# Attention block on one core: 1/l through ScalarE's queue, sums of the second pair made on VectorE, weights in two tiles, division pinned, v's products in seven of eight steps

## The chip, the core and the metric

The kernel runs on one core of a Trainium2 chip. The core has TensorE (PE, matmuls), VectorE (DVE), ScalarE (ACT), GpSimd (POOL) and SyncE (SP); each works through its own queue of instructions in order, and they wait for each other on semaphores. DMAs are issued by SP, ACT and POOL. Everything is fp32. The metric is device time in microseconds, shorter is better.

## What is computed

x has 16 images of 512 channels and 32 x 32 = 1024 positions. Each image is normalised in 8 groups of channels, goes through self-attention with 4 heads of 128 channels, and a projection is added to x:

```
qkv = jnp.einsum('oc,bchw->bohw', qkv_w, xn) + qkv_b[:, None, None]
q, k, v = jnp.split(qkv, 3, axis=1)          # then to heads: b, head, n, d
attn = jax.nn.softmax(jnp.einsum('bhnd,bhmd->bhnm', q, k) * scale, axis=-1)
out = jnp.einsum('bhnm,bhmd->bhnd', attn, v)  # then back to b, c, h, w
out = jnp.einsum('oc,bchw->bohw', proj_w, out) + proj_b[:, None, None]
return x + out
```

## The kernel before

**The main loop.** An image has four heads, a head eight steps (j = 0 to 7), one for each 128 keys. In step s, `scores` (L709) multiplies the keys' block with all queries in two halves of 512 (L712), ScalarE takes exp (L717), VectorE adds the result to `tot` (L723, L725); `weighted_sum` (L792) multiplies the block of step s - 1 with v (L797). There are 16 x 4 x 8 = 512 steps. After a head's last step ScalarE copies the weighted sum out of PSUM (L804).

**The work between.** All other products are laid into the steps as units, by `plan_head` (L938) and `spread`: in head 0 of an image the q and k of its second pair of heads, in head 1 the projection of the image before and the statistics of the next one, in head 2 the first pair's q and k of the next image, in head 3 the next image's v. Half of a step's units run after each half of the scores. Each of the four is a product of 512 by 512 by 1024 done by Strassen's scheme (its Winograd form) on two levels, in `two_levels` (L457): the outer seven products fall into four groups, `OUTER` (L151), of two, two, two and one. Each group has seven units, one for each inner product in the order 1, 2, 6, 5, 7, 4, 3; the groups start 0, 4, 8 and 16 units from the first (`staggered`, L833), so that two are under way at a time. A unit's matmuls are at L510; ScalarE copies intermediate results (L421, L527), VectorE adds them (L529), combines groups (L565) and finishes q and k (L597), v (L649 and L652, then through DRAM on POOL's queue at L660 and L665) and the projection (L693, L696).

**Inner sums.** A group needs four sums of its right-hand factor, t1 to t4 (`inner_sum`, L486; a subtraction of 128 x 256 at L495 for each of the group's members). For the first pair of heads they are made on VectorE and also written to DRAM (`"keep"`, L499). The second pair and v have the same right-hand factor and load them from there through SP's queue (`"load"`, L484, and `first_loads`, L556, for the first group, called as `ahead[...]` one head earlier). The projection makes its own. There is one tile for each of t1 to t4.

**Weights.** `group_weights` (L345) brings the seven left-hand factors of a group, `[128, 2, 7, 128]`, into one of two buffers of the tag `w`; `SLOTS` (L147) says which factor lies where. In the first image they are made from the given weights and written to DRAM (L376), later loaded from there through SP (L350), 896 KB for a group of two.

**1/l.** When a head is done, `denominators` (L727) takes the sums of `tot` over the keys on VectorE (L732 to L742), writes 1/l as one row of 1024 to DRAM (L744) and reads it back spread over 128 partitions (L746), both on SP's queue; the second waits for the first. `divide` (L806) multiplies the head's output with it on VectorE. It is traced in step 5 of the next head. The divided outputs of an image's heads are added up for the projection (`sums_of_b`, L268, traced in step 6 of the next image's head 0). The very last head is divided in another way (L753).

**What sets the order.** The program is traced in the order of the text, then a planner puts each engine's instructions into a queue: an engine takes the instruction traced first among those that the planner's clock holds to be ready. An instruction can thus stand far from where it was traced. `tc.issue_after(ins)` keeps a block's instructions behind `ins` on its engine.

Of the kernel before, what the change touches and what calls it, by code (L numbers as in the profile page):

```python
# [16 lines left out]
P = 128  # L17
# [126 lines left out]
    5: ("s1", "t1"), 6: ("s2", "t2"), 7: ("s3", "t3"),  # L144
}

SLOTS = {"a11": 0, "a12": 1, "a21": 2, "s3": 2, "a22": 3, "s1": 4, "s2": 5, "s4": 6}  # L147
KC = 2
Q = 256

# [4 lines left out]
def fast_path(ctx, tc, x, sources, out, consts, flag, dims):  # L155
# [157 lines left out]
    stage, store = {}, {}  # L313
    for site in (*range(PAIRS), "proj", "v"):
        for g, group in enumerate(OUTER):
            store[site, g] = kept.tile(
                [P, len(group), 7, P], F32, name=f"kept_{site}_{g}"
            )

    store["last"] = kept.tile([P, 8, HALF], F32, name="kept_last")  # L320

# [22 lines left out]

    def group_weights(site, g, first):  # L345

        group = OUTER[g]
        w = wpool.tile([P, 2, 7, P], F32, tag="w", name=f"w_{site}_{g}")
        if not first:
            nc.sync.dma_start(w[:, : len(group)], store[site, g])  # L350
            return w
        st, raw = stage[site], raw_blocks(site)
        for i, p in enumerate(group):
            n = FACTORS[p][0]
            flat = w[:, i, 0:4, :].rearrange("p s d -> p (s d)")
            if n in raw:
                load_block(w[:, i, 0:4, :], raw[n])
            elif n == "s1":
                nc.vector.tensor_add(flat, st["a21"], st["a22"])
            elif n == "s2":  # L360
                nc.vector.tensor_sub(flat, st["s1"], st["a11"])
            elif n == "s3":
                nc.vector.tensor_sub(flat, st["a11"], st["a21"])
            else:
                nc.vector.tensor_sub(flat, st["a12"], st["s2"])
            if site == "proj":
                nc.sync.dma_start(store["last"][:, p], flat)

        def at(n):
            return w[:, : len(group), SLOTS[n], :]  # L370

        nc.vector.tensor_add(at("s1"), at("a21"), at("a22"))
        nc.vector.tensor_sub(at("s3"), at("a11"), at("a21"))
        nc.vector.tensor_sub(at("s2"), at("s1"), at("a11"))
        nc.vector.tensor_sub(at("s4"), at("a12"), at("s2"))
        nc.sync.dma_start(store[site, g], w[:, : len(group)])  # L376
        return w

    wv = {}
# [77 lines left out]
    def two_levels(name, site, b, blocks, finish, sums="make"):  # L457
# [10 lines left out]
        def group_units(g):  # L468
            group = OUTER[g]
            n = len(group)  # L470
            have = haves[g]

            def weights():
                have["w"] = group_weights(site, g, b == 0 and site in range(PAIRS))

            def sum_tile(h, m):
                haves[h][m] = tpool.tile(
                    [P, 2, Q], F32, tag=f"in_{m}", name=f"{name}_{h}_{m}"
                )
                return haves[h][m][:, : len(OUTER[h])]  # L480

            def load(h, m):
                if sums == "load" and h < len(OUTER):
                    nc.sync.dma_start(sum_tile(h, m), inner_kept[b, h, m])  # L484

            def inner_sum(m):  # L486
                if sums == "load":
                    return
                sum_tile(g, m)
                a, c = {  # L490
                    "t1": ("b12", "b11"), "t2": ("b22", "t1"), "t3": ("t2", "b11"),
                    "t4": ("b21", "t2"),
                }[m]
                for i in range(n):
                    nc.vector.tensor_sub(have[m][:, i, :], inner(i, a), inner(i, c))  # L495
                if sums == "keep":
                    t = dpool.tile([P, n, Q], F32, tag=f"{m}_{g}", bufs=1, name=f"kept_{m}_{g}")
                    inner_kept[b, g, m] = t
                    nc.gpsimd.dma_start(t, have[m][:, :n])  # L499

            def inner(i, m):
                if m[0] == "t":
                    return have[m][:, i, :]
                outer = blocks()[FACTORS[group[i]][1]]
                return outer[int(m[1]) - 1][:, ts(int(m[2]) - 1, Q)]

            def mm(acc, j, first):
                an, bn = FACTORS[j]
                for i in range(n):
                    nc.tensor.matmul(  # L510
                        acc[:, ts(i, Q)], have["w"][:, i, SLOTS[an], :], inner(i, bn),
                        start=(first and i == 0), stop=True, skip_group_check=True,
                    )

            def out_(which, a, c=None):
                row, half = int(which[1]) - 1, int(which[2]) - 1
                if g not in R:
                    R[g] = rpool.tile(
                        [P, 2, 2, HALF], F32, tag=f"r{g % 3}", name=f"{name}_r{g}"
                    )  # L520
                dst = R[g][:, :n, row, ts(half, Q)]

                def view(t):
                    return t[:, : n * Q].rearrange("p (i q) -> p i q", q=Q)

                if c is None:
                    nc.scalar.copy(dst, view(a))  # L527
                else:
                    nc.vector.tensor_add(dst, view(a), view(c))  # L529

            p1, p2, p6, p5, p7, p4, p3 = strassen(f"{name}_{g}", mm, out_, n * Q)

            def unit(*steps):
                def one():
                    for f in steps:
                        f()
                    for _ in range(min(len(pending), 2 if g == len(OUTER) - 1 else 1)):
                        pending.pop(0)()
                return one

            def end():
                combine(g)
                if g == len(OUTER) - 1:
                    run(pending)
                    pending.clear()


            return [
                unit(weights, lambda: inner_sum("t1"), lambda: inner_sum("t2"), p1),
                unit(lambda: inner_sum("t3"), p2), unit(lambda: inner_sum("t4"), p6),  # L550
                unit(lambda: load(g + 1, "t2"), p5), unit(lambda: load(g + 1, "t1"), p7),
                unit(lambda: load(g + 1, "t3"), p4),
                unit(lambda: load(g + 1, "t4"), p3, end),
            ]
# [34 lines left out]
    def qk_groups(b, pair):  # L589

        def finish(which, r, a, c):
            of, half = int(which[1]) - 1, int(which[2]) - 1
            st, h = (qs, ks)[of], 2 * pair + r
            if (b, h) not in st:
                st[b, h] = qkpool.tile([P, N], F32, tag=f"qk{of}", name=f"qk{of}_{b}_{h}")
            i = of * HEADS + h
            nc.vector.scalar_tensor_tensor(  # L597
                st[b, h][:, ts(half, HALF)], a, qkb_sb[:, i : i + 1], c, ALU.add, ALU.add
            )

        return two_levels(
            f"qk_{b}_{pair}", pair, b, lambda: xb[b], finish, "load" if pair else "keep"
        )

    def v_units(b, jj):
# [94 lines left out]


    ps, tot, po, rinv, last_eviction = {}, {}, {}, {}, {}
    steps = B * HEADS * NB

    def where(s):
# [3 lines left out]
    def scores(s, half):  # L709
# [11 lines left out]
        if j == 1:  # L721
            tot[b, h] = lpool.tile([P, N], F32, tag="tot", name=f"tot_{b}_{h}")
            nc.vector.tensor_add(tot[b, h], ps[s - 1], ps[s])  # L723
        else:
            nc.vector.tensor_add(tot[b, h][:, i], tot[b, h][:, i], ps[s][:, i])  # L725

    def denominators(b, h):  # L727

# [11 lines left out]
        nc.vector.transpose(l[:, 3, :], l[:, 2, :])  # L740
        r = lpool.tile([BLK, BLK], F32, tag="r", bufs=2, name=f"r_{b}_{h}")
        nc.vector.reciprocal(r, l[:, 3, :])  # L742
        row = dpool.tile([1, N], F32, tag="row", name=f"row_{b}_{h}")
        nc.sync.dma_start(row.rearrange("o (c i) -> (o c) i", i=BLK), r)  # L744
        rinv[b, h] = lpool.tile([P, N], F32, tag="rinv", name=f"rinv_{b}_{h}")
        nc.sync.dma_start(rinv[b, h], row.to_broadcast((P, N)))  # L746
        worst = lpool.tile([BLK, BLK], F32, tag="worst", name=f"worst_{b}_{h}")
        i = b * HEADS + h
        nc.vector.scalar_tensor_tensor(
            worst, l[:, 3, :], 1.0, r, ALU.mult, ALU.max, accum_out=spans[:, i : i + 1]  # L750
        )

    def last_division(b, h):  # L753

# [183 lines left out]
    def plan_head(b, h):  # L938
# [39 lines left out]
        elif h == 2:  # L978
            spread(plan, staggered(qk_groups(b + 1, 0)), 0, NB)
        else:  # L980
            spread(plan, staggered(next_v.pop()), 0, NB)
        return plan

    def warm(n, name):
# [24 lines left out]
    stage_sums(0)  # L1009
    run(staggered(qk_groups(0, 0)))  # L1010
    next_v, next_qk = [], [qk_groups(0, 1)]
    ahead["qk_0_1"]()
    stage_blocks(1)
    stage_sums(1)

# [1 line left out]
    for s in range(steps + 1):  # L1017
        units = []
        if s < steps:
# [4 lines left out]
            if j == NB - 1 and h > 1 and b + 1 < B:  # L1024
                (next_v if h == 2 else next_qk).append(
                    v_groups(b + 1) if h == 2 else qk_groups(b + 1, 1)
                )
                units.append(ahead[f"v_{b + 1}" if h == 2 else f"qk_{b + 1}_1"])
        if 0 < s < steps and s % NB == 0:
            denominators(*where(s - 1)[:2])  # L1030
        for half in range(NH2):
            if s < steps:
                scores(s, half)
                if half == 0 and j == 5 and s > NB:
                    divide(*where(s - NB)[:2])
            if s > 0:
                weighted_sum(s - 1, half)
            n = (len(units) + 1) // 2
# [137 lines left out]
```

## Time and profile before

| | |
|---|---|
| median of 10 runs | 3350.56 us (3344.01 to 3362.43) |
| profiled execution | 3355.27 us, of it the span 3353.4 us |
| granted TensorE clock, mean | 0.986 |
| ACT busy with exp (L717) | 610.0 us, 1024 of 596 ns |
| DVE busy with `tot` (L725) | 469.6 us, 385 of 1220 ns |
| weights, `w`, `w_v` and `w_proj` (SP) | 180 loads of 896 KB, 60 of 448 KB |
| kept sums for q and k (SP) | 192 loads of 256 KB, 64 of 128 KB |
| row of 1/l, its spread (SP) | 63 of 4 KB, 63 of 512 KB |

The profile is of one execution. Busy times of engines overlap; a line of waits gives the engine and line that waited, whom it waited for, the sum, the number and the longest. In a timeline a row gives start, duration, engine, line, what is written from what, the count, and in brackets the idle time before it and what ended it. The line numbers are those of the kernel before.

### The profile page before, as it was taken

The numbers are of one execution on the slowest core, as the hardware profiler recorded it, in microseconds if no ns is written. First come the engines' busy times: TensorE is split into PE (matmuls) and PEld (weight loads), VectorE is DVE, ScalarE is ACT, GpSimd is POOL, SyncE is SP. The second block draws the span as 40 slices with busy tenths as digits, with TensorE's granted clock in tenths as the row PEclk, the third lists the DMA queues.
The fourth block names the chain that finished last, engine by engine and source line by source line (L and its number), as shares of the span: only waits on it lengthen the run. The fifth ranks groups of instructions, "written<-read, shape, count | busy, mean of one in ns | idle before, by whom it ended". The sixth has DMA issues, their size and how long they took to land.

```text
span 3353.4 us, 33635 instructions
## 1 busy us (share of the span) xinstructions
PE 3221.2 (96%) x10474; PEld 2184.3 (65%) x10474; DVE 2520.2 (75%) x4161; ACT 1437.8 (43%) x2709; POOL 526.0 (16%) x938
## 2 busy tenths in 40 slices
PE   8999999999999999999999999999999999999999
PEld 6566666666666666666666666666666666666664
DVE  7876869768687776877778677786776867778675
ACT  2534435344353443534435353353533535344342
POOL 1011121111211112120121201212012121121100
PEclk9999999999999999999999999999999999999999
DMA  6665564555645456464564645646456474464731
GB/s 226 214 201 176 172 210 162 178 162 171 216 152 184 155 183 200 160 190 150 177 204 152 200 152 173 208 146 212 138 171 204 148 217 149 163 201 156 220 130 45
DMA packets 209527, 589.27 MB, mean 176 GB/s; under 512 B 32960, under 2 KB 64192, under 8 KB 209344
## 3 DMA queue, kind: packets, MB, share of 16 engines
q1 hardware_dynamic: 140080, 368.89, 34.5%
q0 software_dynamic: 67392, 216.07, 19.3%
q10 hardware_dynamic: 1872, 2.11, 0.2%
q8 instruction: 86, 1.41, 0.2%
q14 instruction: 97, 0.79, 0.1%
HBM read 448.28 MB, written 138.67 MB: 175 GB/s over the span
## 4 chain that ended last, share of the span: by engine, by line
PE 65%; DVE 13%; DMA 10%; issue 10%; POOL 1%; ACT 0%; SPq 0%; POOLq 0%; ACTq 0%; DVEq 0%
PE po L797 18%; PE s L712 17%; PE qk_x L510 8%; PE qk_y L510 6%; PE v_x L510 5%; PE v_y L510 4%; PE pp_x L510 3%; DMA w<-kept 3%; PE pp_y L510 3%; DMA rinv<-row 2%; DMA row<-r 2%; DVE xt L272 2%; DMA y<-in_x 1%; DVE tot L725 1%; DVE vt L649 1%
## 5 line engine op out<-in xcount | busy, mean ns | idle before, releaser
L717 ACT ACTIVATE p<-s 128x512 f32<-128x512 f32 x1024 | 610.0, 596 | 1072.9 <-PE s L712 1067.2
L797 PE MATMUL po<-p,v 128*128 128x512 f32 x2048 | 1063.2, 601 | 1.2 <-ACT o L804 1.2
L712 PE MATMUL s<-qk,qk 128*128 128x512 f32 x2048 | 1060.4, 600 | 2.2 <-ACT p L717 1.9
L797 PEld LDWEIGHTS po<-p,v 128*128 128x128 f32 x2048 | 602.3, 303 | 332.1 <-issue 215.8
L725 DVE TENSOR_TENSOR tot<-tot,p 128x1024 f32<-128x1024 f32 x385 | 469.6, 1220 | 115.8 <-ACT p L717 113.6
L712 PEld LDWEIGHTS s<-qk,qk 128*128 128x128 f32 x2048 | 391.2, 192 | 93.4 <-issue 29.7
L510 PEld LDWEIGHTS qk_x<-qk_t,w 128*128 128x128 f32 x1344 | 253.0, 193 | 184.7 <-issue 72.3
L510 PE MATMUL qk_x<-qk_t,w 128*128 128x256 f32 x1344 | 361.8, 386 | 7.2 <-ACT qk_u L421 6.0
L529 DVE TENSOR_TENSOR qk_r<-qk_y,qk_u 128x512 f32<-128x512 f32 (+1 forms) x256 | 158.7, 620 | 164.8 <-ACT qk_u L421 139.2
L421 ACT COPY qk_u<-qk_x 128x512 f32<-128x512 f32 (+1 forms) x256 | 136.1, 532 | 260.4 <-PE qk_x L510 260.4
L499 POOL DMA_DIRECT2D kept_t<-qk_t x256 | 138.2, 540 | 490.2 <-DVE qk_t L495 442.2
L510 PE MATMUL qk_y<-qk_t,w 128*128 128x256 f32 x448 | 134.2, 414 | 75.8 <-DVE qk_r L529 69.8
L660 POOL DMA_DIRECT2D vd<-vu x120 | 66.3, 552 | 805.2 <-DVE vu L652 781.1
L807 DVE TENSOR_TENSOR o<-o,rinv 128x1024 f32<-128x1024 f32 x63 | 77.1, 1223 | 135.8 <-DMA rinv<-row 135.4
L510 PE MATMUL pp_x<-pp_t,w_proj 128*128 128x256 f32 x630 | 173.3, 389 | 0.0
L510 PEld LDWEIGHTS v_x<-v_t,w_v 128*128 128x128 f32 x630 | 118.4, 190 | 79.1 <-issue 38.3
L697 POOL DMA_DIRECT2D out_y<-y x120 | 66.2, 551 | 651.7 <-DVE y L696 619.5
L529 DVE TENSOR_TENSOR v_r<-v_y,v_u 128x512 f32<-128x512 f32 (+1 forms) x120 | 74.7, 623 | 123.4 <-ACT v_u L421 115.8
L510 PE MATMUL v_x<-v_t,w_v 128*128 128x256 f32 x630 | 166.6, 381 | 0.0
L510 PEld LDWEIGHTS qk_y<-qk_t,w 128*128 128x128 f32 x448 | 86.7, 202 | 116.4 <-DVE qk_r L529 75.8
L665 POOL DMA_DIRECT2D v<-vd x240 | 139.8, 590 | 104.1 <-issue 44.1
L510 PEld LDWEIGHTS pp_x<-pp_t,w_proj 128*128 128x128 f32 x630 | 113.9, 190 | 63.7 <-issue 18.9
(204 smaller groups left out, 4358.5 us busy)
## 6 DMA issues: line engine op xcount, KB each, us to landing
w<-kept SPq DMA_DIRECT2D x90, 896.0 KB, 6.2
kept_t<-qk_t POOLq DMA_DIRECT2D x192, 256.0 KB, 3.0
qk_t<-kept_t SPq DMA_DIRECT2D x192, 256.0 KB, 4.6
v_t<-kept_t SPq DMA_DIRECT2D x180, 256.0 KB, 2.7
w_v<-kept_v SPq DMA_DIRECT2D x45, 896.0 KB, 4.9
w_proj<-kept_proj SPq DMA_DIRECT2D x45, 896.0 KB, 4.5
rinv<-row SPq DMA_DIRECT2D x63, 512.0 KB, 4.9
x<-in_x POOLq DMA_DIRECT2D x60, 512.0 KB, 6.0
```

The costliest lines, as they stand in the source:

```text
L272: nc.vector.tensor_sub(b[o][k], b[i][k], b[j][k])
L421: nc.scalar.copy(t[n][:, :width], t["x"][:, :width])
L499: nc.gpsimd.dma_start(t, have[m][:, :n])
L510: nc.tensor.matmul(acc[:, ts(i, Q)], have["w"][:, i, SLOTS[an], :], inner(i, bn), start=(first and i == 0), stop=True, skip_group_check=True,)
L529: nc.vector.tensor_add(dst, view(a), view(c))
L660: nc.gpsimd.dma_start(rows[which][ts(h, P), :], u)
L665: nc.gpsimd.dma_start(vs[b, pair][ts(q, BLK), half].rearrange("m h (k i) j -> m (h k) (i j)", k=n), rows[which].rearrange("(k m) (q e) -> ...
L712: nc.tensor.matmul(sc, ks[b, h][:, ts(j, P)], qs[b, h][:, ts(half, HALF)], start=True, stop=True)
L717: nc.scalar.activation(ps[s][:, ts(half, HALF)], sc, AF.Exp, scale=SCALE)
L725: nc.vector.tensor_add(tot[b, h][:, i], tot[b, h][:, i], ps[s][:, i])
L797: nc.tensor.matmul(po[b, h][:, i], v_block(b, h, j), ps[s][:, i], start=(j == 0), stop=(j == NB - 1),)
L807: nc.vector.tensor_mul(os_[b, h], os_[b, h], rinv.pop((b, h)))
```

## The change

- The two DMAs of 1/l leave `denominators` and SP's queue. A new function, `spread_inverse`, issues them on ScalarE's queue: the row is traced in the first half of step 1 of the next head, the spread in the second half.
- `divide` is traced in the second half of step 4 instead of the first half of step 5, and kept behind VectorE's sum of step 4 on `tot`.
- The second pair makes its inner sums on VectorE (`"make"`) instead of loading them; its `ahead` call is gone. The first pair still writes them out, for v.
- A group's weights lie in two tiles, of four factors (a11, a12, s1, s2, which the products 1, 2, 6 and 5 use) and three (a21 or s3, a22, s4, for 7, 4 and 3), with two buffers each, and are stored and loaded in two DMAs. Where the first image makes them, each 512 wide operation becomes two of 256.
- The units of v in head 3 are laid into steps 0 to 6 instead of 0 to 7.

```diff
-SLOTS = {"a11": 0, "a12": 1, "a21": 2, "s3": 2, "a22": 3, "s1": 4, "s2": 5, "s4": 6}
+SLOTS = {
+    "a11": (0, 0), "a12": (0, 1), "s1": (0, 2), "s2": (0, 3),
+    "a21": (1, 0), "s3": (1, 0), "a22": (1, 1), "s4": (1, 2),
+}
+PARTS = (4, 3)
...
-            store[site, g] = kept.tile(
-                [P, len(group), 7, P], F32, name=f"kept_{site}_{g}"
-            )
+            for t, m in enumerate(PARTS):
+                store[site, g, t] = kept.tile(
+                    [P, len(group), m, P], F32, name=f"kept_{site}_{g}_{t}"
+                )
...
-        w = wpool.tile([P, 2, 7, P], F32, tag="w", name=f"w_{site}_{g}")
+        n = len(group)
+        w = [
+            wpool.tile([P, 2, m, P], F32, tag=f"w{t}", name=f"w{t}_{site}_{g}")
+            for t, m in enumerate(PARTS)
+        ]
         if not first:
-            nc.sync.dma_start(w[:, : len(group)], store[site, g])
+            for t in range(2):
+                nc.sync.dma_start(w[t][:, :n], store[site, g, t])
             return w
...
                 for i in range(n):
                     nc.tensor.matmul(
-                        acc[:, ts(i, Q)], have["w"][:, i, SLOTS[an], :], inner(i, bn),
+                        acc[:, ts(i, Q)], have["w"][t][:, i, slot, :], inner(i, bn),
                         start=(first and i == 0), stop=True, skip_group_check=True,
                     )
...
-            f"qk_{b}_{pair}", pair, b, lambda: xb[b], finish, "load" if pair else "keep"
+            f"qk_{b}_{pair}", pair, b, lambda: xb[b], finish, "make" if pair else "keep"
...
-            nc.vector.tensor_add(tot[b, h][:, i], tot[b, h][:, i], ps[s][:, i])
+            added[b, h, j] = nc.vector.tensor_add(
+                tot[b, h][:, i], tot[b, h][:, i], ps[s][:, i]
+            )
...
-        row = dpool.tile([1, N], F32, tag="row", name=f"row_{b}_{h}")
-        nc.sync.dma_start(row.rearrange("o (c i) -> (o c) i", i=BLK), r)
-        rinv[b, h] = lpool.tile([P, N], F32, tag="rinv", name=f"rinv_{b}_{h}")
-        nc.sync.dma_start(rinv[b, h], row.to_broadcast((P, N)))
+        inverse[b, h] = r
...
+    def spread_inverse(b, h, step):
+
+        if step == 0:
+            row = rows_of[b, h] = dpool.tile([1, N], F32, tag="row", name=f"row_{b}_{h}")
+            nc.scalar.dma_start(
+                row.rearrange("o (c i) -> (o c) i", i=BLK), inverse.pop((b, h))
+            )
+            return
+        rinv[b, h] = lpool.tile([P, N], F32, tag="rinv", name=f"rinv_{b}_{h}")
+        nc.scalar.dma_start(rinv[b, h], rows_of.pop((b, h)).to_broadcast((P, N)))
...
-            spread(plan, staggered(next_v.pop()), 0, NB)
+
+            spread(plan, staggered(next_v.pop()), 0, NB - 1)
...
-    ahead["qk_0_1"]()
...
-                units.append(ahead[f"v_{b + 1}" if h == 2 else f"qk_{b + 1}_1"])
+                if h == 2:
+                    units.append(ahead[f"v_{b + 1}"])
...
-                if half == 0 and j == 5 and s > NB:
-                    divide(*where(s - NB)[:2])
+                if j == 1 and s > NB:
+                    spread_inverse(*where(s - NB)[:2], half)
+                if half == 1 and j == 4 and s > NB:
+
+                    with tc.issue_after(added[b, h, 4].ins):
+                        divide(*where(s - NB)[:2])
```

More of the change, by code (lines that the diff above doesn't have):

```diff
@@ L353, in group_weights, with of, at @@
         for i, p in enumerate(group):
[L354 to L365, printed above, removed]
-            if site == "proj":
-                nc.sync.dma_start(store["last"][:, p], flat)
-        def at(n):
-            return w[:, : len(group), SLOTS[n], :]
+            name = FACTORS[p][0]
+            for t in range(2):
+                rows = w[t][:, i, 0:2, :]
+                flat = rows.rearrange("p s d -> p (s d)")
+                if name in raw:
+                    nc.sync.dma_start(
+                        rows, raw[name][:, ts(t, P)].rearrange("(k p) d -> p k d", p=P)
+                    )
+                    continue
+                def of(m):
+                    return st[m][:, ts(t, 2 * P)]
+                if name == "s1":
+                    nc.vector.tensor_add(flat, of("a21"), of("a22"))
+                elif name == "s2":
+                    nc.vector.tensor_sub(flat, of("s1"), of("a11"))
+                elif name == "s3":
+                    nc.vector.tensor_sub(flat, of("a11"), of("a21"))
+                else:
+                    nc.vector.tensor_sub(flat, of("a12"), of("s2"))
+            if site == "proj":
+                for t in range(2):
+                    nc.sync.dma_start(
+                        store["last"][:, p, ts(t, 2 * P)],
+                        w[t][:, i, 0:2, :].rearrange("p s d -> p (s d)"),
+                    )
+        def at(m):
+            t, slot = SLOTS[m]
+            return w[t][:, :n, slot, :]
         nc.vector.tensor_add(at("s1"), at("a21"), at("a22"))
@@ L375, in group_weights @@
         nc.vector.tensor_sub(at("s4"), at("a12"), at("s2"))
-        nc.sync.dma_start(store[site, g], w[:, : len(group)])
+        for t in range(2):
+            nc.sync.dma_start(store[site, g, t], w[t][:, :n])
         return w
@@ L508, in mm @@
                 an, bn = FACTORS[j]
+                t, slot = SLOTS[an]
                 for i in range(n):
                     nc.tensor.matmul(
-                        acc[:, ts(i, Q)], have["w"][:, i, SLOTS[an], :], inner(i, bn),
+                        acc[:, ts(i, Q)], have["w"][t][:, i, slot, :], inner(i, bn),
                         start=(first and i == 0), stop=True, skip_group_check=True,
@@ L702, in fast_path @@
     ps, tot, po, rinv, last_eviction = {}, {}, {}, {}, {}
+    inverse, rows_of, added = {}, {}, {}
     steps = B * HEADS * NB
@@ L724, in scores @@
         else:
-            nc.vector.tensor_add(tot[b, h][:, i], tot[b, h][:, i], ps[s][:, i])
+            added[b, h, j] = nc.vector.tensor_add(
+                tot[b, h][:, i], tot[b, h][:, i], ps[s][:, i]
+            )
     def denominators(b, h):
@@ L751, in denominators @@
         )
+    def spread_inverse(b, h, step):
[3 more added lines that the diff above has]
+                row.rearrange("o (c i) -> (o c) i", i=BLK), inverse.pop((b, h))
+            )
+            return
+        rinv[b, h] = lpool.tile([P, N], F32, tag="rinv", name=f"rinv_{b}_{h}")
+        nc.scalar.dma_start(rinv[b, h], rows_of.pop((b, h)).to_broadcast((P, N)))
     def last_division(b, h):
```

## The prediction

> **What bounds the kernel now.** I read the page first, for the share of each engine, then the windows by head, then the waits, and last the timeline where the waits are.
>
> ```profile
> PE 3221.2 (96%) x10474; PEld 2184.3 (65%) x10474; DVE 2520.2 (75%) x4161; ACT 1437.8 (43%) x2709; POOL 526.0 (16%) x938
> ```
>
> TensorE is the bound: 3353.4 - 3221.2 = 132 us of the span is all that it is idle. The program repeats one image 16 times and an image has four heads, each with the same count of matmuls. Cutting the timeline at the first exp (L717) of each head gives the stretches; those of image 5, heads 0 to 3 in order, are:
>
> ```profile
> core 0: us, PE busy (x) PEld busy (x) DVE busy (x) ACT busy (x) POOL busy (x), PEclk, DMA share, GB/s
> 1077.00:1134.10 57.10, 51.39 (x163) 34.89 (x163) 35.93 (x55) 18.97 (x34) 12.22 (x22) 0.94 0.67 201
> 1134.10:1184.00 49.90, 49.81 (x167) 34.36 (x167) 42.25 (x79) 33.49 (x70) 6.51 (x11) 1.00 0.39 133
> 1184.00:1236.30 52.30, 49.78 (x163) 33.52 (x163) 43.82 (x78) 19.13 (x34) 9.71 (x18) 1.00 0.53 177
> 1236.30:1285.60 49.30, 49.05 (x163) 34.29 (x163) 35.18 (x48) 19.08 (x35) 5.09 (x9) 1.00 0.59 185
> ```
>
> The first number after the stretch is its length. The same work takes 49.3 us in head 3 and 57.1 us in head 0, and only there is the clock below 1. Over images 1 to 14 the means are 56.7, 50.0, 51.4 and 49.2 us. So the time to be had lies in head 0 (7.5 us each) and head 2 (2.2 us). The waits say what it is:
>
> ```profile
> DVE o L807 <- DMA rinv<-row: 135.4, 40, 9.4
> PE qk_y L510 <- DVE qk_r L529: 70.4, 15, 7.5
> PE qk_x L510 <- DMA w<-kept: 20.1, 22, 2.2
> SPq L744 <- DVE worst L749: 249.5, 47, 20.3
> SPq L746 <- DMA row<-r: 111.3, 50, 6.0
> ACT y L866 <- DMA y<-in_x: 11.9, 4, 6.5
> ```
>
> (Columns: total us, times, longest.) VectorE waits for the spread row of 1/l before its division, and TensorE waits 15 times, about once an image, for a sum of products that stands behind that division in VectorE's queue. In image 5:
>
> ```profile
> 1084.65 0.32 SPq L744 DMA_DIRECT2D row<-r  x1
> 1091.48 0.32 SPq L746 DMA_DIRECT2D rinv<-row  x1
> 1096.97 1.22 DVE L807 TENSOR_TENSOR o<-o,rinv 128x1024 f32<-128x1024 f32 x1 [6.41 <-DMA rinv<-row]
> 1100.76 0.68 DVE L529 TENSOR_TENSOR qk_r<-qk_y,qk_u 128x512 f32<-128x512 f32 x1
> 1100.90 2.08 PE L510 MATMUL qk_y<-qk_t,w 128*128 128x256 f32 x4 [4.49 <-DVE qk_r L529]
> ```
>
> The 4 KB row takes 6.8 us to land and the 512 KB spread another 5.5; the division stands at the head of VectorE's queue for 6.41 us, and TensorE stops for 4.49. After it the clock is low:
>
> ```profile
> 1077.00:1098.00 21.00, 18.20 (x62) 12.50 (x61) 10.64 (x19) 8.22 (x14) 10.16 (x19) 1.00 0.84 228
> 1098.00:1106.00 8.00, 5.10 (x10) 2.93 (x11) 4.51 (x7) 0.60 (x1) 0.99 (x2) 0.57 1.03 331
> 1106.00:1134.00 28.00, 28.00 (x93) 19.36 (x92) 20.68 (x30) 10.16 (x19) 1.06 (x2) 1.00 0.43 144
> ```
>
> (Second last number but one: granted clock, then the DMA engines' share.) The stall sits where the DMA engines are full, and the clock falls to 0.57 with it.
>
> [...] every stall of 3.3 us or more in a head 0 has a half-clock stretch of 3.4 to 10.2 us beside it, and the waits of 1.6 to 2.2 us in head 2 have none. [...] the row's landings on SP: 1.3 us median in heads 1 and 3, 2.1 in head 2, and 3.7 to 6.8 in head 0, where weights and kept sums lie ahead of it. [...]
>
> **The change part by part.** Durations are from the profiled execution, which took 3355.3 us (span 3353.4), 4.7 us above the median of 3350.6; the sum is made against it and taken over to the median by those 4.7.
>
> *1/l through ScalarE, division pinned.* The two DMAs of a head leave SP and go to ACT, traced at step 1; the division can't come before VectorE's sum of step 4. In a head 0, exp of step 1 ends at 7.9 us after its start and r is ready at 7.7. With about 2.1 us for the row and 5 for the spread, 1/l is there by some 16 us; the pin stands at about 30. So VectorE's wait goes, TensorE's with it, and the half clock too. Next late in that head is the weights' load (1.21 us at 1086.68), which the second part moves. Head 0 then looks like head 2 without its weights' wait: 51.4 - 1.6 (its mean idle) = 49.8, so 6.9 us each. In image 15 TensorE stalls 5.32 us in head 0 for another reason (ACT in L866 waits 6.5 us for y), which the change leaves. So 14 x 6.9 = 97 us. The sums of o for the projection follow the division, and even at 38 us they stand ahead of the projection of the next head.
>
> The cost: ACT's issue of the spread waits until the row has landed, and its issue of the row until r is there; exps and the copies of L421 stand behind, and TensorE waits for those. SP's issues take 0.32 us each; the trace has four ACT issues of x at 0.41 to 0.46, so two a head are below 1 us of an engine that is busy 19 to 33 us of 50. The wait isn't shown. Below: nothing, if the row lands before ACT gets there (half a step, about 3 us, lies between the two). Above: what the trace shows of a blocked ACT, 6.5 us of wait in image 15 gave 5.3 us of stall, so some 1.2 us are forgiven and the rest is paid in full. For a wait of up to 2.1 us that is at most 0.9 a head. I take 0.2 for 62 heads, 12 us, since 1.3 to 2.1 is less than half a step.
>
> *Sums of the second pair made.* Gone are 16 loads an image on SP (3.5 MB, all for head 0, just where the DMA engines were full). Added are 28 subtractions in head 0; L495 has them for the first pair at 412 ns, so 28 x 0.41 = 11.5 us of VectorE. [...] Head 0's VectorE goes from 36.0 to 47.5, less what v's tail takes along (L649 and L652 have 3.6 us in head 0): 44 to 47.5. Head 2 makes the same sums with 43.8 us and shows waits of TensorE for them of 5.9 us in 14 times over the run, so below 0.5 an image. I take nothing for it beyond the 49.8; the upper bound is in the rivals.
>
> *Weights in two tiles.* The bytes are the same; 16 more SP issues an image cost SP 5 us of 207, beside the 16 loads that go. The first tile (four products) is free after the fourth product of the group two before, three products earlier than the whole was, and 4/7 of it has to land: it comes 3 units (over 2.5 us) earlier, against waits of at most 2.2. So head 2's mean idle of 1.6 goes: 15 x 1.6 = 24 us. Head 0's is in the 49.8. If SP issues a second tile ahead of a first one, part of it stays.
>
> *v's products within seven of eight steps.* Nothing is added. Step 7 of head 3 then has scores and weighted sums alone, some 3.4 us (4 x 0.86); VectorE gets the 3.6 us of v's tail over before head 0. I put 0.2 on head 3 for the uneven filling, 3 us in all. The preparation of the first image makes its sums in halves of 0.41 instead of 0.68: 1 us.
>
> Sum: - 97 - 24 + 12 + 3 + 1 = - 105, or 3250 against 3355.3, 3246 against the median.
>
> **The rivals.** *VectorE becomes head 0's bound.* For: 47.5 of 49.8 us. Head 2 leaves VectorE 6 us unused outside its weights' wait (49.8 - 43.8); if so much is always lost to waits for products, head 0 takes 53.5: 15 x 3.7 = 55 us more, 3300. Against: v's tail leaves head 0, and head 1 can take what is late.
>
> *The change doesn't do what it says.* The stall lies where DMA share is 1.03; if the spread comes late there too, or VectorE only meets another wait (y<-in_x, L693, 14.2 us in all), half of the 121 goes: about 3305. Against it, the pin lies 8 us after the latest landing seen in a head 0 (21.5).
>
> *Slower: ScalarE waits for the row.* In head 2, r is ready at 11.5 us, exp of step 1 ends at 5.6: if ACT issues in the order of the text, it stands 5.9 us, and 5.9 - 1.2 = 4.7 reach TensorE, 15 x 4.7 = 70. In head 0, the row at SP's 5.1 us gives 3.9, 15 x 3.9 = 58. Heads 1 and 3 (r at 5.4 and 4.9) give none. [...] 30 half-clock stretches of 3.4 us add 1.7 each, 51. In place of my 12: 3246 - 12 + 179 = 3413. It decides from 105 + 12 = 117 us on, 1.9 us a head. Against it: the order of this kernel's queues is a planner's (L807, traced at step 5, stands at step 2 or 3), so ACT's issues may be put where r is expected[...].
>
> **How the numbers follow.** The forecast has 0.58, VectorE's bound 0.18, the half effect 0.10, ScalarE's wait 0.12, no net effect 0.02. A measurement of this kernel can tell about 0.2%, 7 us, from no change. Faster 0.58 + 0.18 + 0.10 = 0.86, same 0.02, slower 0.12. The likeliest case goes from 3212 (both heads at 49.2 and no ACT wait: 14 x 7.5 + 15 x 2.2 = 138) to 3275; the range reaches to 3320 to take in the two smaller gains and leaves ScalarE's wait out.
>
> **What would show it.** Right: no division waits for rinv, head 0 at 50 us with clock 1.00, the row landing in about 2 us on ACT's queue, no TensorE wait for w, VectorE 44 to 47 us in head 0. Wrong: ACT waiting for row or r with TensorE idle behind exp or the copies; TensorE waiting for qk_t or qk_r in head 0 by more than 1 us an image; head 3 longer than 50.

## The result, and the profile after

The changed kernel takes 3298.86 us (median of 9 runs, 3293.81 to 3309.37), against 3349.9 us for the kernel before (31 runs, beside it on the same chips). The ratio is 0.9847, 95% interval 0.9836 to 0.9859: 51 us faster, where 105 were forecast. The profiled execution took 3300.64 us, its span is 3298.9 us. Page, shares of the engines:

```profile
PE 3202.4 (97%) x10474; PEld 2178.3 (66%) x10474; DVE 2639.8 (80%) x4625; ACT 1444.0 (44%) x2709; POOL 525.1 (16%) x938
```

The stretches of image 5, heads 0 to 3, as shown of the kernel before:

```profile
core 0: us, PE busy (x) PEld busy (x) DVE busy (x) ACT busy (x) POOL busy (x), PEclk, DMA share, GB/s
1066.80:1120.10 53.30, 50.93 (x163) 34.42 (x163) 43.38 (x77) 18.68 (x34) 11.20 (x21) 0.97 0.55 156
1120.10:1169.70 49.60, 49.22 (x165) 34.10 (x165) 41.86 (x83) 34.15 (x70) 6.00 (x11) 1.00 0.39 123
1169.70:1224.40 54.70, 51.98 (x165) 34.97 (x165) 44.81 (x80) 19.07 (x35) 10.24 (x19) 0.97 0.53 179
1224.40:1274.10 49.70, 49.08 (x163) 34.14 (x163) 34.73 (x50) 19.26 (x35) 6.86 (x12) 1.00 0.55 175
```

Head 0 has fallen, but not to 50, and head 2 has not fallen (this one is the longest of its kind). The means over images 1 to 14 are 52.6, 49.7, 51.75 and 49.7 us, against 56.7, 50.0, 51.4 and 49.2. The waits of the changed kernel that answer to those of before (division and exp now at L846 and L746, the matmuls of the units at L538):

```profile
ACT qk_u L448 <- DVE worst L777: 47.0, 14, 3.6
...
ACT p L746 <- DVE qk_t L522: 42.8, 16, 4.5
...
PE qk_x L538 <- DVE qk_t L522: 38.4, 30, 3.3
...
ACT qk_p L448 <- DMA row<-r: 25.4, 8, 6.1
...
DVE qk_t L522 <- DMA kept_t<-qk_t: 15.6, 23, 2.3
...
PE qk_y L538 <- DVE qk_r L557: 12.7, 15, 2.3
```

The division waits for its row no more, and TensorE has no wait for w of 0.3 us or more in images 1 to 14. In their place TensorE waits for inner sums, and ScalarE for VectorE and for the row. Image 5 where head 3 passes into head 0:

```profile
1070.49 1.22 DVE L763 STREAM_TRANSPOSE tt<-tot 128x1024 f32<-128x1024 f32 x1
...
1071.63 1.04 DVE L680 STREAM_TRANSPOSE vu<-vt 128x512 f32<-128x512 f32 x1
1072.51 1.17 DVE L765 TENSOR_REDUCE part<-tt 128x32 f32<-128x1024 f32 x1
...
1073.59 0.42 DVE L522 TENSOR_TENSOR qk_t<-x,qk_t 128x256 f32<-128x256 f32 x1
...
1074.15 1.47 PE L538 MATMUL qk_x<-qk_t,w 128*128 128x256 f32 x4 [2.26 <-DVE qk_t L522]
...
1075.46 1.81 PE L741 MATMUL s<-qk,qk 128*128 128x512 f32 x2
...
1076.02 0.33 ACTq L785 DMA_DIRECT2D row<-r  x1
...
1082.63 0.33 ACTq L790 DMA_DIRECT2D rinv<-row  x1
```

VectorE is at work without a pause; the sum that TensorE needs stands behind a transpose of v's tail and the denominators of the head before. TensorE stops for 2.26 us and then, in this image, runs at half clock (0.50 granted from 1075.56 to 1078.97 us; 1.81 us for two matmuls that take 1.02 elsewhere). And the row, on ScalarE's own queue, still takes 6.5 us to land, with ScalarE's issue of the spread behind it.

### The profile page after: what moved, and what is told of

Same layout as the page of the kernel before. It is cut to its first block, busy times and chain, and to the rows that moved or that the text cites. A ratio compares the mean times of both kernels' runs of the same rounds, so it can differ in the third digit from the quotient of the medians.

```text
span 3298.9 us, 34096 instructions
## 1 busy us (share of the span) xinstructions
PE 3202.4 (97%) x10474; PEld 2178.3 (66%) x10474; DVE 2639.8 (80%) x4625; ACT 1444.0 (44%) x2709; POOL 525.1 (16%) x938
## 4 chain that ended last, share of the span: by engine, by line
PE 39%; issue 36%; DVE 12%; DMA 8%; POOL 5%; POOLq 0%; ACTq 0%; ACT 0%; SPq 0%; DVEq 0%
PE po L836 11%; PE s L741 10%; PE qk_x L538 6%; DMA vd<-vu 4%; PE qk_y L538 4%; POOL kept_t L526 4%; PE pp_x L538 3%; PE pp_y L538 3%; DMA out_y<-y 2%; DVE xt L277 2%; DMA y<-in_x 1%; DVE vu L680 1%; DVE tot L754 1%; DVE part L765 1%; DVE tt L763 1%
## 5 line engine op out<-in xcount | busy, mean ns | idle before, releaser
L746 ACT ACTIVATE p<-s 128x512 f32<-128x512 f32 x1024 | 609.7, 596 | 856.1 <-PE s L741 806.5
L538 PE MATMUL qk_x<-qk_t,w 128*128 128x256 f32 x1344 | 363.9, 387 | 42.5 <-DVE qk_t L522 38.4
L538 PEld LDWEIGHTS qk_x<-qk_t,w 128*128 128x128 f32 x1344 | 248.9, 191 | 212.7 <-issue 108.2
L538 PE MATMUL pp_x<-pp_t,w_proj 128*128 128x256 f32 x630 | 170.7, 387 | 6.4 <-ACT pp_p L448 6.4
L538 PE MATMUL v_x<-v_t,w_v 128*128 128x256 f32 x630 | 166.6, 381 | 0.0
L538 PEld LDWEIGHTS pp_x<-pp_t,w_proj 128*128 128x128 f32 x630 | 113.9, 190 | 76.3 <-issue 22.5
L538 PE MATMUL qk_y<-x,w 128*128 128x256 f32 x512 | 143.7, 382 | 12.4 <-DVE qk_r L557 12.4
L538 PEld LDWEIGHTS v_x<-v_t,w_v 128*128 128x128 f32 x630 | 118.5, 190 | 53.6 <-issue 23.0
L448 ACT COPY v_u<-v_x 128x512 f32<-128x512 f32 (+1 forms) x124 | 66.2, 534 | 165.3 <-PE v_x L538 124.7
L752 DVE TENSOR_TENSOR tot<-p,p 128x1024 f32<-128x1024 f32 x64 | 78.3, 1223 | 74.5 <-ACT p L746 74.5
```

The lines of the kernel that those rows point to most:

```text
L448: nc.scalar.copy(t[n][:, :width], t["x"][:, :width])
L538: nc.tensor.matmul(acc[:, ts(i, Q)], have["w"][t][:, i, slot, :], inner(i, bn), start=(first and i == 0), stop=True, skip_group_check=True,)
L746: nc.scalar.activation(ps[s][:, ts(half, HALF)], sc, AF.Exp, scale=SCALE)
```

## The experiments

Each was timed in five rounds beside the kernel before; ratios carry 95% intervals. The median of the kernel before moved between 3346.7 and 3351.9 us from set to set, so that runs of different sets are compared by their ratios. Head lengths are means over images 1 to 14 of the one profiled execution. "Loss" is, per head, the time between the starts of neighbouring matmuls beyond 0.215 us for 256 columns and 0.43 for 512 (the medians in the traces of before and after are 0.216 and 0.429); it holds the half clock too. "Largest part" is the share of it that a wait for the thing named makes up, without the half clock that follows.

| run | us | ratio to before | heads 0, 1, 2, 3 | loss in head 0, and its largest part |
|---|---|---|---|---|
| before | 3349.9 | | 56.7, 50.0, 51.4, 49.2 | 8.1; 5.2 sum behind the division |
| after | 3298.9 | 0.9847 (0.9836 to 0.9859) | 52.6, 49.7, 51.75, 49.7 | 3.9; 2.8 inner sum, VectorE |
| e1_load | 3385.7 | 1.0103 (1.0081 to 1.0126) | 57.3, 50.2, 51.8, 50.3 | 8.6; 6.3 copy on ScalarE |
| e2_sp | 3301.9 | 0.9857 (0.9837 to 0.9877) | 53.1, 49.7, 51.8, 49.7 | 4.4; 2.8 inner sum, VectorE |
| e3_pin | 3395.8 | 1.0131 (1.0110 to 1.0153) | 59.0, 49.7, 52.2, 49.4 | 10.3; 7.8 weights |
| e4_onew | 3293.5 | 0.9823 (0.9800 to 0.9847) | 52.0, 49.6, 51.5, 49.7 | 3.3; 2.3 inner sum, VectorE |
| e5_v8 | 3295.5 | 0.9841 (0.9824 to 0.9857) | 52.1, 49.7, 51.8, 49.6 | 3.5; 2.4 inner sum, VectorE |
| e6_make | 3309.6 | 0.9886 (0.9871 to 0.9901) | 53.4, 50.0, 51.4, 49.4 | 4.7; 2.1 sum behind the division |
| e7_both | 3338.4 | 0.9972 (0.9961 to 0.9983) | 52.2, 49.7, 53.9, 49.7 | 3.4; 2.7 inner sum, VectorE |
| e8_mix | 3351.4 | 1.0013 (1.0005 to 1.0021) | 55.3, 49.7, 52.1, 50.3 | 6.6; 4.4 copy on ScalarE |
| e9_mix_sp | 3255.5 | 0.9726 (0.9709 to 0.9743) | 48.8, 49.7, 51.6, 50.3 | 0.1 |
| e10_load_sp | 3356.0 | 1.0025 (1.0015 to 1.0035) | 55.3, 49.8, 51.85, 50.3 | 6.6; 4.3 loaded sum |
| e11_traffic | 3306.1 | 0.9872 (0.9854 to 0.9889) | 53.1, 49.7, 51.7, 49.7 | 4.4; 2.9 inner sum, VectorE |
| e12_allmake | 3271.7 | 0.9769 (0.9751 to 0.9787) | 51.6, 49.6, 51.25, 49.7 | 2.9; 2.1 inner sum, VectorE |
| e13_mix_v8 | 3236.1 | 0.9664 (0.9645 to 0.9684) | 48.8, 49.7, 51.5, 49.4 | 0.1 |
| e14_mix_onew | 3302.2 | 0.9853 (0.9831 to 0.9876) | 51.9, 49.6, 52.3, 50.3 | 3.2; 2.1 weights |
| e15_mix_vmake | 3246.5 | 0.9698 (0.9678 to 0.9718) | 48.8, 49.6, 51.8, 49.55 | 0.1 |

**The division alone.** The kernel before, with `divide` traced in step 4 and kept behind `tot`'s sum:

```diff
-                if half == 0 and j == 5 and s > NB:
-                    divide(*where(s - NB)[:2])
+                if half == 1 and j == 4 and s > NB:
+                    with tc.issue_after(added[b, h, 4].ins):
+                        divide(*where(s - NB)[:2])
```

> The kernel before with one edit: the division is traced in step 4 and kept behind VectorE's sum of that step. Theory (the stall of head 0 is the division's place alone, since 1/l lands 21.5 us after the head's start at the latest and the pin stands near 30): head 0 loses 8.1 - 6.5 = 1.6 us instead of 8.1, the half clock goes, 14 x 6.5 = 91 us, 3350 - 91 = 3259 us. Rival (the queue matters, the row and the loads behind it on SP are late): less than half of that, above 3305 us.

3395.8 us: slower than before. The division's wait is gone, and TensorE's longest waits are now, in the waits and in image 5:

```profile
PE qk_x L510 <- DMA w<-kept: 134.2, 33, 9.6
```

```profile
1117.69 2.07 PE L510 MATMUL qk_x<-xt,w 128*128 128x256 f32 x4 [6.20 <-DMA w<-kept]
```

Neither theory had this. The load that is late is that of the third group. In the kernel before the same load was just as slow, and no wait showed it:

```profile
1093.86 0.32 SPq L350 DMA_DIRECT2D w<-kept  x1
...
1106.64 1.03 PE L510 MATMUL qk_x<-xt,w 128*128 128x256 f32 x4
```

It landed 11.2 us after its issue, at 1105.0, 1.6 us ahead of the matmuls that use it, because TensorE had stood 4.49 us for the division and run at half clock after it (0.50 granted from 1098.53 to 1105.36). With that stall gone the matmuls are due sooner, the load (10.8 us in this run) is not, and TensorE loses 7.8 us a head. It is not the load behind the wait of 1.21 us that the prediction names: that one is the second group's, issued before the head began.

**The changed kernel with the sums loaded.** `"make"` is `"load"` again, with its `ahead` call; first on ScalarE's queue, then with both DMAs of 1/l on SP:

```diff
-            f"qk_{b}_{pair}", pair, b, lambda: xb[b], finish, "make" if pair else "keep"
+            f"qk_{b}_{pair}", pair, b, lambda: xb[b], finish, "load" if pair else "keep"
...
-        nc.scalar.dma_start(rinv[b, h], rows_of.pop((b, h)).to_broadcast((P, N)))
+        nc.sync.dma_start(rinv[b, h], rows_of.pop((b, h)).to_broadcast((P, N)))
```

> The changed kernel, but the second pair's inner sums are loaded again as before, with the first group's loads one head earlier. Theory (VectorE is late with the made sums of the first group at the start of head 0, behind v's tail and the denominators): TensorE's wait for qk_t in step 0 of head 0 goes, 2.8 us an image, head 0 falls from 52.6 to some 50, the kernel to 3299 - 15 x 2.8 = 3257 us. Rival (it is ScalarE, waiting for r and for the row, that holds head 0; or the loads fill the DMA engines again and cost as much): 3292 to 3310 us, and head 0 stays above 52.

> As the run with all sums of the second pair loaded (3386 us), but 1/l on SP's queue. Theory (with the 3.5 MB in head 0 the DMA engines are full and some wait shows whatever the queue; without ScalarE in it, it is less than 8.6 us a head): 3320 to 3380 us, with the wait in another place (the loaded sums, w or v). Rival (ScalarE's queue was the whole of it): 3260 us or below. The two tiles of weights are worth something here if TensorE's wait for w stays under the 7.8 us that the pinned kernel before had.

3385.7 us, slower than both texts had it, and 3356.0 us, as the theory had it. The first is the change without its made sums: 1.0% slower than the kernel before. With loads and ScalarE's queue, image 5 shows the whole chain:

```profile
1098.25 0.32 ACTq L785 DMA_DIRECT2D row<-r  x1
...
1105.85 0.33 ACTq L790 DMA_DIRECT2D rinv<-row  x1
1106.21 0.59 ACT L448 COPY qk_u<-qk_x 128x512 f32<-128x512 f32 x1 [6.94 <-DMA row<-r]
...
1106.85 2.08 PE L538 MATMUL qk_x<-qk_t,w 128*128 128x256 f32 x4 [5.37 <-ACT qk_u L448]
```

The row is 7.6 us on its way; the issue of the spread waits for it, a copy of 0.59 us waits behind the issue, and of ScalarE's 6.94 us TensorE pays 5.37. On SP no copy stands behind that issue, and TensorE's wait is another one, for the loaded sums:

```profile
PE qk_x L538 <- DMA qk_t<-kept_t: 61.6, 15, 5.7
```

So with the loads there, mending one wait in head 0 shows another: weights in the pinned kernel before, loaded sums or what ScalarE has behind the row in these two.

**The sums made, alone.** The kernel before with `"make"`, division, queues and weights untouched:

```diff
-            f"qk_{b}_{pair}", pair, b, lambda: xb[b], finish, "load" if pair else "keep"
+            f"qk_{b}_{pair}", pair, b, lambda: xb[b], finish, "make" if pair else "keep"
```

> The kernel before with one edit: the second pair's sums made instead of loaded; division, queues and weights as before. Theory (the DMA engines, full in the first 28 us of head 0, are the cause, and every wait there is only where it shows; 3.5 MB an image less in that stretch is what the change brought): most of the change's gain, 3295 to 3320 us, with the division's wait in head 0 below 4 us. Rival (the pinned division brought the gain, the made sums alone add 11.5 us of VectorE in head 0): 3345 us or more.

3309.6 us: 1.14% of the change's 1.53%, by the edit on which I had put no gain. The division still stands in VectorE's way, but for less, and TensorE already waits for made sums:

```profile
DVE o L807 <- DMA rinv<-row: 100.0, 39, 8.3
...
PE qk_y L510 <- DVE qk_r L529: 33.1, 17, 4.8
...
PE qk_y L510 <- DVE qk_t L495: 28.3, 28, 1.5
```

Head 0 loses 3.3 us less. TensorE's waits there fall from 5.2 to 3.4 us; the rest is in the main half clock, of which there are 4 stretches in images 1 to 14 instead of one in each image (mean granted clock 0.996 for 0.986). The row, issued at the same place on SP (7.6 us for 7.7 in the median), lands after 1.8 us instead of 4.9, but the spread then takes 8.3 instead of 6.5, so that 1/l is there only 1.4 us sooner (17.9 for 19.3 us in the mean).

**Traffic without anyone waiting.** The same bytes read into unused DRAM beside the made sums; in the second run each copy is kept behind its group's weights on SP's queue:

```diff
+            with tc.issue_after(loads[-1].ins):
+                nc.sync.dma_start(t, inner_kept[b, h, m])
```

> The changed kernel, its sums made on VectorE, and beside that the same 16 loads an image issued by SP where they were, into memory that nobody reads (DRAM[...]), so that traffic comes without anyone waiting for it. Theory (traffic is the cause): head 0 goes back to 55 us or more, with the row of 1/l at 7 us or more and ScalarE standing behind it, 3345 to 3400 us. Rival (waiting for loaded sums was the cost, or the removed SP issues): within 8 us of 3299.

> The changed kernel, sums made, and the same bytes as the 16 loads read by SP into DRAM that nobody uses, each kept behind the weights' load of its own group on SP's queue, so that it falls into head 0 (in the run without that it had moved into head 2). Theory (traffic in head 0 is the cause, not the wait on loaded data): head 0 from 52.6 to 56 us or more, the row and spread of 1/l later, 3350 to 3400 us. Rival (traffic is harmless, head 0 needs somebody who waits for loaded sums): within 10 us of 3299.

In the first, nothing held the copies in place and the planner put them into head 2, which grew from 51.75 to 53.9 us; of head 0 it says nothing. In the second, of 224 copies in images 1 to 14, 140 lie in head 0, none of them before 18.7 us, and 84 in the last 13 us of head 3. The DMA engines are busy for 0.91 of the first 28 us of head 0, against 0.75 in the changed kernel and 0.95 in the kernel before, and it costs little: 3306.1 us, the interval overlapping that of the changed kernel. So bytes at that place are not the cause by themselves (these were moved from DRAM to DRAM). What copies beside the row would do is not shown: the row has landed, by 16.6 us, when the first one in head 0 is issued. That the cost lies in transfers which somebody needs soon after they can first be issued is my reading; no run here isolates it.

**ScalarE or SP for 1/l.** In the changed kernel, both DMAs of 1/l on SP:

> The changed kernel, but the row of 1/l and its spread are issued by SP, traced at the same places; the pin stays. Theory (the pin alone keeps VectorE free, and ScalarE's waits for r and the row are nearly all forgiven): within 8 us of 3299. Rival (ScalarE's waits, 115 us in 38 times in the trace of the changed kernel, reach TensorE but for 1.2 us each): 3299 - 70 = 3230 us. A third (the row needs ScalarE's queue to come in time): VectorE waits for rinv again at the pin, over 3320.

3301.9 us, not to be told from the changed kernel. It would be wrong to read from this that ScalarE's waits are free: they lie under VectorE's lateness, for TensorE is already some 3.9 us late in head 0 when it needs what stands behind the row. That shows when the lateness is taken away. The sums of the first group are loaded one head earlier and the other three groups' made, on ScalarE's queue and then on SP's:

```diff
-                if sums == "load":
+                if sums == "load" or (sums == "mix" and g == 0):
                     return
```

> The changed kernel with the sums of the second pair's first group loaded one head earlier (1 MB) and those of the other three made. Theory (VectorE's lateness in step 0 is what is left in head 0, 2.8 us of wait and 0.9 of half clock): 3299 - 15 x 2.8 = 3257 us. Rival (even 1 MB there delays the row of 1/l and v, and ScalarE stands behind the row): 3290 us or more.

> As the run with the first group's sums loaded and the others made (3351 us), but 1/l on SP's queue. Theory (there ScalarE stood 3 to 6 us behind the row in head 0 with its copies behind it, 4.4 us of TensorE's loss; SP can stand without harm, the pin leaves time, and VectorE's lateness in step 0 is gone): head 0 loses under 2 us, 3255 to 3280 us. Rival (the 1 MB of loads keeps the DMA engines full, and another wait takes the place, w or v): 3320 us or more.

3351.4 against 3255.5 us: the queue of two small DMAs is worth 96 us here. On ScalarE, TensorE's wait behind it is

```profile
PE qk_x L538 <- ACT qk_u L448: 61.1, 16, 5.2
```

and on SP head 0 has no stall left: 48.8 to 49.1 us in images 1 to 14, and the mean granted clock of the run is 0.999.

**Weights in one tile, v over eight steps.** Undone one at a time, in the changed kernel and in the one at 3255.5 us:

```diff
+        whole = wpool.tile([P, 2, 7, P], F32, tag="w", name=f"w_{site}_{g}")
+        w = [whole[:, :, 0:4, :], whole[:, :, 4:7, :]]
...
-            spread(plan, staggered(next_v.pop()), 0, NB - 1)
+            spread(plan, staggered(next_v.pop()), 0, NB)
```

> The changed kernel with a group's weights in one tile of seven and one load again. Theory (the two tiles took the waits for w away, 1.4 us an image in head 2): TensorE waits for w again in head 2 and the time is 3299 + 15 x 1.4 = 3320 us. Rival (in the changed kernel VectorE's waits in step 2 of head 2 stand in the same place, and a wait for w only hides behind them): within 8 us of 3299.

> As the run at 3255 us, but a group's weights in one tile of seven. Theory (the two tiles keep TensorE from waiting for w in heads 0 and 2, hidden before by other stalls): 3270 us or more, with a wait for w of 1 us an image or more. Rival (nothing hangs on them here either): within 7 us of 3255.

> The changed kernel with v's units laid into eight steps again. Theory (VectorE is the late one in step 0 of head 0, and v's tail, 4.2 us of it, goes back there): TensorE's wait for qk_t there grows by 2 to 4 us an image, 3330 to 3360 us. Rival (the planner sets the order anew and v's last sums are no obstacle; head 3 gets back its 0.4 us): 3285 to 3300 us.

> As the run at 3255 us (first group's sums loaded, others made, 1/l on SP), but v's units laid into eight steps. Theory (seven steps cost 1.1 us a head 3, 1.72 of loss against 0.59 in the kernel before, and VectorE has room in head 0 now): 3255 - 15 x 1 = 3240 us. Rival (v's tail goes to head 0, VectorE is late there again): 3265 us or more.

In the changed kernel neither can be told from nothing (3293.5 and 3295.5 us, intervals overlapping). With one tile, head 2 has its waits for w back (1.4 us an image) and those for VectorE are gone: the one hid behind the other. With head 0 mended, the two tiles are worth 43 us by the ratios, and without them TensorE waits again:

```profile
PE qk_x L533 <- DMA w<-kept: 56.3, 30, 5.3
```

v over eight steps then gains some 20 us: head 3 falls from 50.3 to 49.4, 0.9 x 15 = 14, and head 0 stays at 48.8. This is the fastest version run, 3236.1 us, 3.4% below the kernel before. Its stretches of image 5:

```profile
1048.50:1097.20 48.70, 48.70 (x163) 34.21 (x163) 42.17 (x72) 19.03 (x34) 13.06 (x24) 1.00 0.63 197
1097.20:1146.80 49.60, 49.22 (x165) 34.09 (x165) 41.97 (x83) 33.73 (x70) 6.15 (x11) 1.00 0.37 124
1146.80:1198.30 51.50, 50.48 (x165) 33.97 (x165) 44.63 (x80) 19.16 (x35) 10.09 (x19) 1.00 0.55 189
1198.30:1247.70 49.40, 49.18 (x163) 34.18 (x163) 33.09 (x46) 19.16 (x35) 5.00 (x9) 1.00 0.56 176
```

The DMA share of its head 0 (0.63) is hardly below that of the kernel before (0.67), at 8 us less: here busy DMA engines were no stall by themselves.

**No sums kept at all.** v makes its own too; in the changed kernel without any stores, in the one at 3255.5 us with those of the first group alone:

```diff
-        return two_levels(f"v_{b}", "v", b, lambda: xb[b], finish, "load")
+        return two_levels(f"v_{b}", "v", b, lambda: xb[b], finish)
```

> The changed kernel with v's inner sums made as well, so that none is kept or loaded: 3.5 MB of stores in head 2 and 3.5 MB of loads in head 3 go for each image, VectorE gets 11.5 us more in head 3 (34.5 of 49.7 us before). Theory (bytes cost more here than VectorE's time): head 2 loses its wait behind the kept stores, about 1 us an image, the row of 1/l lands sooner in head 0; head 3 holds: 3260 to 3290 us. Rival (VectorE is late at the seam of heads 3 and 0 already and is now later): above 3310 us, with the wait for qk_t in step 0 of head 0 over 4 us.

> As the run at 3255 us, but v makes its inner sums too, and the first pair stores only those of its first group. Theory (head 2 loses 2.5 us an image to the stores that hold its sums' tiles; head 3 has the room): head 2 falls by 0.5 to 1.5 us, 3235 to 3250 us. Rival (VectorE gets 11.5 us in head 3 and is late at the seam to head 0): 3265 us or more.

3271.7 and 3246.5 us. The first is 0.8% faster than what it starts from, and in part by the mechanism that I gave: the row of 1/l lands sooner in head 0 (at 13.1 us for 15.3 in the median), head 3 holds, and head 2 falls, but by 0.5 us instead of 1; the larger gain, 1.0 us an image, is in head 0. The second is 9 us faster, with intervals that overlap a little, and not by that mechanism: its head 2 rose by 0.2, and the gain lies in head 3 (50.3 to 49.55). With no stores at all head 2 still takes 51.25 us, so they are not what holds it. What keeps head 2 at 51.5 us, with VectorE late for qk_r and qk_t in its step 2, stays open.

## Why the prediction was wrong

- **Right: direction and place.** The division's wait and the stall of 3.4 to 7.5 us behind it are gone, the division runs 12 to 21 us after the mean landing of 1/l, and head 0 carries the gain. VectorE in head 0 is at 43.3 us, below the foreseen 44 to 47.5.
- **Failed: the step "1/l through ScalarE, division pinned", 97 us, which ends with head 0 "like head 2 without its weights' wait".** I took the stall for the work of one wait and named one successor (weights, 1.21 us, another load than the one that came). The pinned division alone made the kernel 44 us slower: it uncovered weights, 7.8 us a head; with two weight tiles and the sums still loaded, the loss was 4.3 us for the loaded sums with 1/l on SP, and 6.3 behind ScalarE's issue with 1/l on ACT. The trace of before had what was needed to see it: weights issued in head 0 land up to 13 us after their issue, and the prediction priced the landings of the row and the spread alone.
- **Failed: "I take nothing" for the made sums.** Two errors of opposite sign. They were the edit that brought most (37 us alone; without them the rest of the change loses 1.0%); and they put VectorE late in the first 7 us of head 0, which costs TensorE 2.8 us an image, 3.9 with the half clock. I weighed VectorE's 43 to 47 us against the whole head's 50 instead of against the stretch in which the first sums are needed. Head 0 came to 52.6 for 49.8: 14 x 2.8 = 39 us short, the largest part of the 54 that are missing.
- **Failed: "head 2's mean idle of 1.6 goes", 24 us.** The wait for w went, and VectorE's sums of step 2 took its place, 1.7 us of loss. Head 2 is 0.3 us longer than before, not 1.6 shorter: 15 x 1.9 = 29 us short.
- **Mis-sized: the row on ScalarE's queue at 2.1 us.** It took 5.3 to 7.4 us in head 0. The 12 us that I charged for ScalarE were not paid in the changed kernel, where SP in its place saves nothing (e2_sp), because VectorE was later still. That they were not paid is luck: the rival that ended slower, ScalarE waiting for the row, is what e1_load and e8_mix show; it was held off by VectorE's lateness, not by the place of the issues.
- **The seven steps.** Head 3 is 0.4 us longer than before (0.2 foreseen), but eight steps give back only 0.1 of it in the changed kernel (e5_v8), so the rest is not theirs. Where head 0 is clean they cost 0.9.

That the row would land in about 2 us once it left SP's queue was my estimate, and no trace had shown it. At the same place of the changed kernel the row took 6.1 us in the median on ACT's queue and 7.5 on SP's (e2_sp): ScalarE's queue gave 1.4 us, and did not spare it the rest.

## What to carry to other kernels

Where one wait is seen in a stretch with slow transfers, list every transfer that is needed there, with issue, landing and need, before crediting the mending of the first: others may be late behind it without a wait that shows it (in e3_pin the weights, 7.8 us a head). A DMA that must wait for another belongs on a queue with nothing urgent behind it (the spread behind the row: 3351.4 us on ScalarE's queue in e8_mix, 3255.5 on SP's in e9_mix_sp). And undo parts in a version without other stalls: here the same part read as nothing in one version and as 43 us of gain in another.

## What the runs showed of the hardware

- How long the row of 4 KB takes in head 0 is not set by the issuing queue alone. On SP, issued near 7.7 us after the head's start, it took 3.7 to 6.8 us in the kernel before; issued near 7.6 us in e6_make, without the loaded sums and just ahead of eight DMAs of v on POOL's queue that begin near 8 us, 1.8 us (13 of 15). Issued at 9.0 to 10.8 us it took 5.3 to 7.4 us on ACT in the changed kernel, 6.4 to 9.2 on SP in e2_sp; on SP in e9_mix_sp, at 8.0 to 10.0 us, 4.5 in the median. Which of the other transfers delays it was not isolated.
- The length of a stall alone did not tell whether the clock fell: in the changed kernel, waits of 2.0 to 3.3 us in step 0 of head 0 came with a stretch of 3.4 us at a granted clock of 0.50 in 7 of images 1 to 14, and without one in the other 7; waits of 2.16 us are among both. In the kernel before, waits of 1.6 to 2.2 us in head 2 had none.
